# Two layers of graph aggregation on one core: the idle products of the opening changed in form and number, one product by W.T and one addition of the last stage moved

## The chip, the cores and the metric

The kernel runs on one core of a Trainium2 chip. The metric is the device time of one execution in microseconds (us), as the median of three runs; lower is better. The engines are named as the profile names them: PE is the matrix engine (PEld is its weight load), DVE the vector engine, ACT the scalar engine, POOL the third elementwise engine, SP the engine that only issues transfers here. L373 is line 373 of the kernel.

## The reference

`x` is 4096 x 512, `adj` 4096 x 4096 (sparse, diagonal set, never negative), `W` 512 x 512, all float32. Cut to what is computed:

```python
# layer 0
head = (adj > 0); head = head / max(sqrt(row_sum(head * head)), 1e-12)
inc  = adj + head
x    = layernorm(x + (inc @ x) / row_sum(inc))
# layer 1
A2     = adj + I
dscale = diag(A2) ** -0.5
temp   = A2 @ x @ W.T
A_norm = dscale[:, None] * A2 * dscale[None, :]
x      = layernorm(x + relu(A_norm @ temp))
```

The heavy work is three products of a 4096 x 4096 matrix with a 4096 x 512 one: `inc @ x`, `A2 @ x` and `A_norm @ temp`.

## The kernel before, in words

**Tiling and stages.** Blocks are 128 wide, and everything stays in float32. Each heavy product is done by seven half-size products in place of eight (the sums of operands that this needs are made by DVE). Layer 0 takes one such level, layer 1 two. There are 16 pairs of row blocks in layer 0. The first pair is different: the operand sums of `x` are not there yet, so `multiply_plain` (L542) does its products one by one while the inputs are still landing; the pairs after it go through `multiply1` (L529). Layer 1 is a list of 224 steps, of eight steps for each of seven outer products, two column strips and two multiplications (`steps`); each step issues the seven inner products of `multiply2` (L298), and the last step of eight hands the sums to `inner` and `outer`. The order of the work is written out by hand: the program is emitted in the order in which it is to run (`manual_schedule`), and each engine runs its instructions in that order.

**The opening.** SP issues four half loads of the transposed adjacency block `adj_q` (L615), one for each of the chunks c = 0 to 3. For each chunk `count_half` has ACT take the signs (L353; in the last chunk DVE does half, L367), and PE sums them over the partitions by eight products with a matrix of ones, `ones_b` (L373, 128 columns of bf16 each, all accumulated in PSUM bank 7). ACT then takes the root of the count (L357), DVE finishes the scale (L388, L389) and builds the entries of `inc` from it (`to_inc`, L502 and L504), and only then can the first product of `multiply_plain` run. Between the chunks, `idle_products` has PE do products whose result nobody reads: it takes PSUM bank 2 as a new tile for each one, `bank(2)`, so that each such product gets the bank when the product before it has given it back. The number after each chunk is a list by hand, `(0, 3, 0, 5)`. Their moving operand is a piece of the tile of the features that POOL has filled with ones (L621). The loads of `x` (`load_x`, L336 and L337) stand behind one small POOL copy that reads the signs of chunk 0 (L627), and SP issues them one after the other. The signs go to tiles with two buffers (`sr`), so the signs of chunk c + 2 wait for the counts of chunk c.

**The product by W.T.** Once an eighth of a column block of `A2 @ x` is complete, `project` multiplies it by W.T, also by seven small products of 256 columns. It is a generator: it yields a dictionary from place to action, and `multiply2` runs the action of place m just ahead of its inner product m. One project is spread over three steps. The small product (`product`, two matmuls of K = 128, each of which PE runs as two records, L832) takes the one spare PSUM bank, 7, and ACT copies it out (L834); the next small product needs that bank back. The sums `s1` to `s4` of the operands are made by POOL (L839 to L842). Of every two projects that run together, the second (`first` is false) does its products at other places than the first. In the step whose number is 5, `leave_operands` of the project before runs at the places 2 and 4: ACT scales the rows (L881) and issues their stores (L885, L891).

**The last stage.** `finish` does the last four steps of the seventh outer product with its epilogue woven in. `multiply` runs one inner product over the four steps (L996), `quarter` transposes four blocks of a sum by PE (L1000), has DVE add and clip them (`take`, L1008) and measures them (L1011). `deviation` (L1025 on DVE, L1027 on ACT), `invert` (L1030, L1031 on DVE) and `leave` (L1038 on ACT or L1040 on DVE, and a store by SP, L1042) normalise the rows and store them. `add(c21[:, 3, :], acc[q7])` and `add(c21[:, 2, :], acc[q7])` are two DVE additions (L761) of the inner product q7 into two blocks of the last sum; `quarter(1, 1, 1)` transposes the first of them, and `end_rows` (L1085) reads the second. `begin_rows` (L1082) are the products of the last inner product that come between.

## Time and profile before

| | us |
|---|---|
| median of three runs | 2268.39 (2268.12 to 2269.62) |
| the profiled execution, its own time | 2268.52 |
| its span, first to last instruction | 2266.7 |
| PE busy in the span | 2251.2 (99%) |
| DVE busy | 1846.9 (81%) |
| ACT busy | 538.9 (24%) |
| POOL busy | 298.2 (13%) |
| first idle product starts | 8.22 |
| first product of `multiply_plain` starts | 14.58 |

The profile is one execution. A timeline row gives the start, the time from the first start to the last end of the merged group, engine, line, operation, output<-inputs, shape and count; the bracket at the end is the idle time of the engine ahead of it and what ended it. A float32 product of PE shows as two records. The start of one record to the start of the next is what PE is held; the end of a record holds a pipeline's length more, so the durations of neighbours overlap. "PE q L832 <- ACT p L834" in the table of waits means that PE, at line 832, waited for ACT's instruction that writes p at line 834.

### The profile page before, as it was taken

The page shows a single profiled execution, that of the slowest core. Times are in us where ns is not written, and L with a number is a line of the kernel's source. Part 1 is how long each engine was busy: PE and PEld are TensorE (multiplying, and loading weights), DVE is VectorE, ACT ScalarE, POOL GpSimd, SP SyncE. Part 2 cuts the span into 40 slices and gives each one's busy share as a digit, 9 for nine tenths or more (in the row PEclk, how much of TensorE's full clock was granted, in tenths as well). Part 3 has the DMA queues.
Part 4 walks back from the last instruction along what each step waited for, and adds up shares of the span by engine and source line. Part 5 has one row for each costly group of instructions (what it writes and reads, how often), then busy time and mean ns, then how long its engine had stood idle before and what let it go on. Part 6 is the DMA issues. An engine that isn't in the chain of part 4 may idle for free.

```text
span 2266.7 us, 22289 instructions
## 1 busy us (share of the span) xinstructions
PE 2251.2 (99%) x7409; PEld 1387.3 (61%) x7410; DVE 1846.9 (81%) x2629; ACT 538.9 (24%) x1343; POOL 298.2 (13%) x408
## 2 busy tenths in 40 slices
PE   8999999999999999999999999999999999999998
PEld 7888888888888844444555544555544444444444
DVE  6989999989989886888877888887666789767678
ACT  4346546545553000000111100111110011200013
POOL 0111122221112110001112200111310010100001
PEclk9999999999999999999999999999999999999999
DMA  9778888888886575575677767577775677765674
GB/s 309 262 268 288 264 272 276 287 280 285 266 251 224 184 278 220 205 308 192 239 272 232 231 236 274 177 286 276 217 245 218 235 287 282 254 243 211 234 287 172
DMA packets 177044, 568.29 MB, mean 251 GB/s; under 512 B 18064, under 2 KB 54944, under 8 KB 138528
## 3 DMA queue, kind: packets, MB, share of 16 engines
q1 hardware_dynamic: 128832, 459.32, 57.1%
q0 software_dynamic: 32480, 92.85, 13.1%
q10 hardware_dynamic: 15616, 14.69, 2.0%
q8 instruction: 59, 0.97, 0.2%
q14 instruction: 57, 0.47, 0.1%
HBM read 443.04 MB, written 123.74 MB: 250 GB/s over the span
## 4 chain that ended last, share of the span: by engine, by line
PE 91%; DVE 5%; DMA 3%; issue 1%; ACT 0%; SPq 0%; ACTq 0%; POOL 0%; DVEq 0%
PE q L298 54%; PE q L529 32%; PE q L832 4%; DVE s L170 1%; DMA a<-adj_q 1%; DVE r L255 1%; PE q L996 1%; DMA nat<-adj 1%; DMA a<-adj_r 1%; DMA b<-x 1%; PE q L906 1%; DVE s L172 1%; ACT nat L353 0%; DVE ts L273 0%; DVE c L790 0%
## 5 line engine op out<-in xcount | busy, mean ns | idle before, releaser
L298 PE MATMUL q<-s,ts 128*128 128x512 f32 x1320 | 609.6, 592 | 0.2 <-DVE u L752 0.2
L529 PE MATMUL q<-b,s 128*128 128x256 f32 (+1 forms) x1920 | 453.6, 379 | 0.2 <-DVE s L172 0.2
L298 PEld LDWEIGHTS q<-s,ts 128*128 128x128 f32 x1320 | 250.8, 190 | 294.0 <-issue 268.0
L170 DVE TENSOR_TENSOR s<-a 128x1024 f32<-128x1024 f32 x234 | 288.0, 1231 | 164.8 <-PE q L298 138.8
L529 PEld LDWEIGHTS q<-b,s 128*128 128x128 f32 x1920 | 363.2, 189 | 52.0 <-DVE s L172 0.6
L529 PE MATMUL q<-b,a 128*128 128x256 f32 (+1 forms) x1440 | 350.6, 379 | 0.0
L298 PE MATMUL q<-a,tr 128*128 128x512 f32 x688 | 326.7, 593 | 0.0
L529 PEld LDWEIGHTS q<-b,a 128*128 128x128 f32 x1440 | 273.1, 190 | 37.9
L298 PE MATMUL q<-s,tr 128*128 128x512 f32 x440 | 224.8, 592 | 0.0
L298 PEld LDWEIGHTS q<-a,tr 128*128 128x128 f32 x688 | 129.0, 190 | 144.0 <-issue 137.6
L353 ACT ACTIVATE nat<-nat,tiny 128x512 f32<-128x512 f32 x240 | 172.9, 721 | 29.4 <-DMA nat<-adj 23.1
L298 PE MATMUL q<-a,ts 128*128 128x512 f32 x344 | 176.0, 593 | 0.0
L172 DVE TENSOR_TENSOR s<-a,s 128x512 f32<-128x512 f32 x234 | 165.1, 706 | 8.0
L173 DVE TENSOR_TENSOR s<-a,s 128x512 f32<-128x512 f32 x234 | 164.7, 704 | 8.0
L750 ACT COPY p<-q 128x512 f32<-128x512 f32 x27 | 15.7, 583 | 649.3 <-PE q L298 649.3
L504 DVE TENSOR_TENSOR a<-a,mask 128x1024 f32<-128x1024 f32 (+1 forms) x127 | 154.5, 1217 | 6.4
L502 DVE SCALAR_TENSOR_TENSOR mask<-a,sc 128x1024 f32<-128x1024 f32 (+2 forms) x129 | 154.2, 1196 | 2.2
L298 PEld LDWEIGHTS q<-s,tr 128*128 128x128 f32 x440 | 83.7, 190 | 94.8 <-issue 85.0
L414 ACT ACTIVATE nat<-nat 128x512 f32<-128x512 f32 x192 | 118.4, 617 | 13.1 <-DMA nat<-adj 13.1
L298 PEld LDWEIGHTS q<-a,ts 128*128 128x128 f32 x344 | 65.3, 190 | 80.7 <-issue 75.7
L839 POOL TENSOR_TENSOR y<-c,c 128x256 f32<-128x256 f32 x16 | 21.3, 1334 | 641.3 <-DVE c L765 391.5
L170 DVE TENSOR_TENSOR s<-r 128x1024 f32<-128x1024 f32 x48 | 59.8, 1245 | 40.2 <-PE q L298 32.5
(221 smaller groups left out, 2124.1 us busy)
## 6 DMA issues: line engine op xcount, KB each, us to landing
a<-adj_r SPq DMA_DIRECT2D x112, 1024.0 KB, 7.0
a<-oa SPq DMA_DIRECT2D x80, 1024.0 KB, 5.4
nat<-adj SPq DMA_DIRECT2D x240, 256.0 KB, 6.0
a<-adj_q SPq DMA_DIRECT2D x60, 1024.0 KB, 6.3
tr<-ob SPq DMA_DIRECT2D x112, 512.0 KB, 4.0
oa<-r SPq DMA_DIRECT2D x32, 1024.0 KB, 10.1
oa<-sr POOLq DMA_DIRECT2D x60, 512.0 KB, 7.0
y<-x POOLq DMA_DIRECT2D x64, 256.0 KB, 4.9
```

The costliest lines, as they stand in the source:

```text
L170: nc.vector.tensor_add(s[:, S3:S1 + 1, :], a[:, A11:A22 + 1, :], a[:, A21, :].unsqueeze(1).to_broadcast([P, 2, w]))
L172: nc.vector.tensor_add(s[:, S2, :], a[:, A11, :], s[:, S1, :])
L173: nc.vector.tensor_add(s[:, S4, :], a[:, A12, :], s[:, S2, :])
L255: raises.append(lambda: nc.vector.tensor_add(r, r, a))
L298: nc.tensor.matmul(acc[m], left, right, start=(kk == 0), stop=(kk == last))
L353: nc.scalar.activation(y, a, AF.Sign, bias=tiny, scale=2.0 ** 64, accum_out=accum)
L414: nc.scalar.activation(nat, nat, AF.Copy, accum_out=totals[j][:, h, t:t + 1])
L502: nc.vector.scalar_tensor_tensor(m, v, 0.0, s.unsqueeze(1).to_broadcast(list(v.shape)), op0=ALU.is_gt, op1=ALU.mult)
L504: nc.vector.tensor_add(z, z, y)
L529: nc.tensor.matmul(acc[m][:, 0:w], left, b[:, right, 0:w], start=(kk == 0), stop=(kk == NP - 1))
L832: nc.tensor.matmul(ps, left[:, e, :], wt[:, right, e, :], start=(e == 0), stop=(e == 1))
L906: nc.tensor.transpose(ps[:, at + i * P:at + (i + 1) * P], C_of[3][h][d // 2][:, 2 * r + d % 2, cols], ident)
```

## The change

The idle products are done on `ones_b` for both operands, with 128 columns in place of 512, into the first 128 columns of the bank. There are 30 of them ahead of the first chunk, and after the four chunks 2, 10, 0 and 24 in place of 0, 3, 0 and 5. `ones_b` is now filled by DVE and not by POOL, and POOL's fill of the piece of the features is gone. In the second project of a pair, the product of `s2` with T2 moves from place 5 to place 6. In the last stage, the addition into block 3 moves ahead of `invert` and the four stores of `leave`.

```diff
-    nc.gpsimd.memset(ones_b, 1.0)
+    nc.vector.memset(ones_b, 1.0)
...
     def idle_products(times):
         for _ in range(times):
-            nc.tensor.matmul(bank(2), ones_b, idle, start=True, stop=True)
+            nc.tensor.matmul(bank(2)[:, 0:P], ones_b, ones_b, start=True, stop=True)
...
     ps = spare()
-    nc.gpsimd.memset(feats[-1][:, 1, T2, 0:H], 1.0)
-    idle = feats[-1][:, 1, T2, 0:H].bitcast(BF16)
+    idle_products(30)
     for c in range(NC):
         m = count_half(0, c, ps)
...
-        idle_products((0, 3, 0, 5)[c])
+        idle_products((2, 10, 0, 24)[c])
...
-            yield {1: product(a12, B21), 3: product(a22, T4), 5: product(s2, T2)}
+            yield {1: product(a12, B21), 3: product(a22, T4), 6: product(s2, T2)}
...
         deviation(0, 0, 4)
+        add(c21[:, 3, :], acc[q7])
         invert(0, 0, 4)
         for n in range(4):
             leave(0, n, True)
-        add(c21[:, 3, :], acc[q7])
         add(c21[:, 2, :], acc[q7])
```

## The prediction, made before the changed kernel was run

> **What bounds the kernel now.** I read the engines' busy times first, then the busy time by stretch, then PE's waits.

> ```profile
> PE 2251.2 (99%) x7409; PEld 1387.3 (61%) x7410; DVE 1846.9 (81%) x2629; ACT 538.9 (24%) x1343; POOL 298.2 (13%) x408
> ```
> ```profile
> 0.00:14.58 14.58, 7.24 (x40) 4.28 (x41) 2.62 (x7) 6.02 (x7) 2.92 (x31) 1.00 0.86 271
> 14.58:73.70 59.12, 58.89 (x270) 50.27 (x271) 46.80 (x54) 22.18 (x55) 2.00 (x3) 1.00 0.95 326
> 73.70:1000.00 926.30, 926.30 (x3828) 725.39 (x3829) 810.27 (x1138) 350.23 (x943) 147.52 (x214) 1.00 0.77 259
> ```

> The columns are the length of the stretch, then PE, PEld, DVE, ACT and POOL. From 14.58 us, where the first product of layer 0 starts, PE is never idle for more than parts of a us. The table of PE's waits after 14.6 us agrees: 0.5 us for ACT at L832 in two waits, three of 0.2 us, and the 0.6 us ahead of that first product. The chain of waits names loads for most of the time up to 73.7 us, but there PE waits 0.2 us for them, so PE and the loads are equally late and PE has no slack to give away. The end is therefore the moment at which PE starts L542, plus its stream, plus the last stage. What the idle products do to that moment decides.

> ```profile
> 8.22 1.92 PE L379 MATMUL q<-b,ones_b 128*128 128x512 bf16 x3
> 9.93 1.91 PE L373 MATMUL q<-sr,ones_b 128*128 128x128 bf16 x16
> 11.64 2.34 PE L379 MATMUL q<-b,ones_b 128*128 128x512 bf16 x5
> 11.88 0.37 ACT L357 ACTIVATE sc<-q,half_m 128x128 f32<-128x128 f32 x1 [1.49 <-PE q L373]
> ```
> ```profile
> 8.91 0.58 PE L379 MATMUL q<-b,ones_b 128*128 128x512 bf16 x1
> 9.55 0.58 PE L379 MATMUL q<-b,ones_b 128*128 128x512 bf16 x1
> 12.31 0.38 PE L379 MATMUL q<-b,ones_b 128*128 128x512 bf16 x1
> 12.74 0.38 PE L379 MATMUL q<-b,ones_b 128*128 128x512 bf16 x1
> 34.78 1.03 PE L373 MATMUL q<-sr,ones_b 128*128 128x512 bf16 x4
> ```

> Two things are to be seen. **The clock:** 16 counts of 128 columns at 9.93 us are (1.91 - 0.31)/15 = 0.107 us apart (0.31 is one such record), 1.2 columns per ns; four counts of 512 at 34.78 us are (1.03 - 0.38)/3 = 0.217 us apart, 2.4 columns per ns. The trace's record of the granted clock begins at 12.10 us: until then PE ran at half speed, although it had been working since 6.24 us. **The waits:** idle products of 512 columns are 9.55 - 8.91 = 0.64 us apart at the slow clock, where their columns take 4 x 0.107 = 0.43, and 12.74 - 12.31 = 0.43 us apart at the fast one, where the columns take 0.217. Each spends 0.21 us beyond its columns at either clock. The counts, which add into one tile, do not; the idle products, of which each takes bank 2 anew, start only when the one before has ended.

> **The idle products.** The new ones keep `bank(2)` for each product, so I keep the 0.213 us: one costs 0.107 + 0.213 = 0.32 us at the slow clock and 0.054 + 0.216 = 0.27 us at the fast one. Bounds: 0.107, if nothing waited, and 0.64, the old product. Cross-check: a record of 128 columns by itself takes 0.26 us (the first count, at 6.24) and the next idle product starts 0.06 us after the end of the last (9.49 to 9.55).

> The start: DVE has nothing to do before 9.70 us, and ACT and SP issue their first work at 0.72. DVE's fill has no row; I take 0.2 us from POOL's 0.23 for the same tile (between 0.1 and 0.3), 0.05 from its end to the weight load and 0.03 to the matmul, as at 2.52 and 14.55: first product at 1.0.

> Slow clock throughout, starts in us: 30 products from 1.0, the last at 1.0 + 29 x 0.32 = 10.28; the eight counts of chunk 0 from 10.39 (before: 6.24); two products at 11.24 and 11.56; counts of chunk 1 from 11.67; ten products from 12.52 to 15.40; 16 counts from 15.51 to 17.11 (before, the last at 11.53: 5.58 later); 24 products from 17.22 to 24.58; L542 at 24.69. Meanwhile ACT and DVE need 14.58 - 11.53 = 3.05 us from the last count to the data of L542, so 20.16: PE is late, not they. **L542 starts 24.69 - 14.58 = 10.1 us later.**

> Queued behind the waits: the signs of chunk 2 need the buffer of chunk 0, so ACT waits to 11.3 and DVE and ACT for chunk 3 to 12.6; with 1.15 and 0.72 us of signs all are done by 13.4, before PE asks at 15.51. SP's loads of `x` hang on the signs of chunk 0 alone and stay where they are. POOL's two dropped fills (0.23 and 0.34 us) lay in 3.4 us of idle time ahead of L627: nothing gained.

> Then the clock. An idle product streams 0.107 of 0.32 us, a third. The trace shows the clock lifted after 5.86 us (6.24 to 12.10) in which columns streamed for about 5.1, and no stretch at a third. I take it that a third does not lift it, and that L542 starts slow. Its stream runs at half speed until the lift: at most 5.86 us, a loss of 2.9; at least 0, if it was lifted before. I take 2.0. [...]

> What comes back: with everything else early, small stalls of PE vanish that hung on loads, ACT and DVE up to 73.7 us. From one record's start to the next they are 0.08 and 0.11 longer than usual at 16.2 to 16.5 us (DVE at L504), 0.21 at 32.2 (ACT's signs), 0.33 and 0.10 at 73.2 to 73.7 (L172): 0.8 us together. DVE starts 5.6 us late against PE's 10.1 and is busy 46.8 of 59.1 us there: it stays ahead.

> **The product by W.T.**

> ```profile
> 1082.53 0.59 PE L298 MATMUL q<-s,ts 128*128 128x512 f32 x1
> 1082.87 0.37 ACT L834 COPY p<-q 128x256 f32<-128x256 f32 x1 [1.13 <-issue]
> 1083.39 1.10 PE L832 MATMUL q<-wt,y 128*128 128x256 f32 x4 [0.26 <-ACT p L834]
> ```

> The product at place 5 finds bank 7 still unread: ACT has two scalings and three store issues ahead of the copy. From 1082.53 to 1083.39 is 0.86 us where a record holds PE 0.43; with 0.07 on the next record, 0.50. The same at 1468.67: 0.47. One place later is two records, 0.86 us: PE would ask at 1083.82, after the copy's end at 1083.24. Both stalls go: **-1.0 us**. Next late is ACT's copy of the moved product, two inner matmuls (1.72 us) ahead of the next small product, the distance that pairs there already have without a stall. The other six such projects stand without a wait now and pay nothing.

> **The last stage.**

> ```profile
> 2253.29 0.61 DVE L1025 BATCH_NORM_AGGREGATE mv<-st 128x2 f32<-128x24 f32 x4
> 2254.45 0.18 DVE L1030 RECIPROCAL sd<-sd 128x4 f32<-128x4 f32 x1 [0.55 <-ACT sd L1027]
> 2254.74 1.28 DVE L761 TENSOR_TENSOR c<-c,q 128x512 f32<-128x512 f32 x2
> 2255.48 0.66 PE L1000 MATMUL q<-ident,c 128*128 128x128 f32 x4 [0.21 <-DVE c L761]
> 2256.17 0.76 DVE L1008 SCALAR_TENSOR_TENSOR o<-q,y 128x256 f32<-128x256 f32 x2 [0.15 <-PE q L1000]
> ```

> The moved addition falls into DVE's 0.55 us of waiting, but q7's last matmul ends only at about 2254.38. So it runs 2254.4 to 2255.0; the reciprocal and L1031 follow to 2255.4, the second addition to 2256.03. PE's L1000 comes at 2255.1, and L1008 starts at 2256.03 in place of 2256.17: **-0.14 us**, between -0.4 and 0. ACT's four scalings (2.93 us) start 0.55 later and end at 2258.4, before ACT's next work at 2258.8; SP's four stores move with them, well ahead of its last ones.

> **The sum.** 10.1 + 2.0 - 0.8 - 1.0 - 0.1 = +10.2 us on the profiled execution's 2268.5, which stands 0.1 above the median of the runs: **2278.6 us** for the median. With the loss at the clock from 1.0 to 2.9 and the small terms off by half: 2277 to 2280.

> **The rivals.**
> A, the forecast: the clock stays low through the idle products. 0.60.
> B, the products wait for each other, but they lift the clock, after 5.86 us as the counts did, at 6.9 us: then 18 at 0.32 and 12 at 0.27, counts from 9.8, two products, counts to 11.0, ten to 13.5, 16 counts to 14.4, and 24 x 0.27 to 20.7: L542 6.1 us later, not slow itself. 6.1 - 0.8 - 1.1 = +4.2: 2272.6 (2272 to 2273.5). For it: by the records' durations PE looks 0.26/0.32 = 81% busy. Against it: 6.24 to 8.7 us streamed 87% and did not suffice. 0.27.
> C, the other side, faster: the products do not wait for each other. The point is the spacing: 30 products fit into 6.24 - 1.0 = 5.24 us at up to 0.17 us each, and 24 into the 2.74 us from the last count to L542 at up to 0.114. At 0.107 both fit and delay nothing; if they also lift the clock, the last counts run in half the time and L542 starts up to 0.9 us earlier. With -1.1 from the two moves: 2266.4 to 2267.3. Against it: the 0.21 us at both clocks above. 0.10.
> Slower still, by something that I do not see: 0.03.

> **How the numbers follow.** The range takes in A and B, which hold 0.87: 2271.0 to 2281.0. What a measurement of this kernel can tell from no change is about 0.2%, 4.5 us: A is above that bound (2272.9), B on it, split 0.12 above and 0.15 within; C is 0.09 within and 0.01 beyond. Faster 0.01, same 0.24, slower 0.75.

> **What would show it.** In the changed kernel's trace: L379 records of 128 columns 0.32 us apart (C: 0.107; B: 0.27 from about 7 us on); the first count at about 10.4 us in place of 6.24; the last idle product at about 24.6 and L542 just behind it, its first records 0.43 us apart in place of 0.217; no wait at L832 near 1083 and 1468 us; L761 ahead of L1030 in the last stage. PE idle for long between 24.7 and 73.7 us would show that the start was not what counts, and the prediction wrong.

## The result, and the profile after

The changed kernel takes 2280.28 us (median of five runs, 2279.25 to 2280.53); the kernel before, five runs beside it, 2268.59. The ratio is 1.005, with a 95% interval of 1.0039 to 1.0062: slower, by 11.7 us. The profiled execution took 2279.3 us, its span 2277.5.

First the page's line of busy times and the busy time by stretch (length, then PE, PEld, DVE, ACT, POOL), the stretches cut where L542 and L529 start.

```profile
PE 2265.3 (99%) x7468; PEld 1393.0 (61%) x7468; DVE 1847.4 (81%) x2630; ACT 538.8 (24%) x1343; POOL 297.8 (13%) x406
```
```profile
0.00:24.86 24.86, 20.29 (x99) 10.34 (x99) 7.37 (x13) 6.02 (x7) 2.53 (x29) 1.00 0.95 306
24.86:84.53 59.67, 59.67 (x268) 51.12 (x268) 47.16 (x54) 21.39 (x51) 2.91 (x4) 1.00 0.78 268
84.53:1010.80 926.27, 926.27 (x3831) 724.64 (x3830) 804.91 (x1132) 350.77 (x946) 146.59 (x213) 1.00 0.76 259
```

The reader is to see that PE is "busy" for 14 us more than before, of which nearly all is in the first stretch, and that from 24.86 to 1010 us it does not stop at all. Busy is not yet useful: the opening, by PE's timeline:

```profile
1.04 9.57 PE L379 MATMUL q<-ones_b 128*128 128x128 bf16 x30 [1.04 <-DVE ones_b L318]
10.41 1.06 PE L373 MATMUL q<-sr,ones_b 128*128 128x128 bf16 x8
11.26 0.63 PE L379 MATMUL q<-ones_b 128*128 128x128 bf16 x2
11.69 1.06 PE L373 MATMUL q<-sr,ones_b 128*128 128x128 bf16 x8
12.54 3.19 PE L379 MATMUL q<-ones_b 128*128 128x128 bf16 x10
15.53 1.91 PE L373 MATMUL q<-sr,ones_b 128*128 128x128 bf16 x16
17.23 7.67 PE L379 MATMUL q<-ones_b 128*128 128x128 bf16 x24
24.86 15.40 PE L542 MATMUL q<-b,a 128*128 128x258 f32 x61
```

Thirty idle products take 9.57 us, (9.57 - 0.26)/29 = 0.32 apart, while eight counts of the same shape take 1.06. The counts of chunk 0, which came at 6.24, come at 10.41, and L542 comes at 24.86 in place of 14.58.

Where the 10.8 us between the two profiled spans lie, by the starts of the first records of each line and, for the last stage, of the second group of transposes at L1000 (L999 after the change):

| stretch | before | after | difference | forecast |
|---|---|---|---|---|
| to L542 | 14.58 | 24.86 | +10.28 | +10.1 |
| L542 to L529 | 57.92 | 59.67 | +1.75 | +2.0 - 0.4 |
| L529 to L298 | 727.02 | 726.58 | -0.44 | -0.4 |
| L298 to the transposes | 1451.66 | 1450.82 | -0.84 | -1.0 |
| transposes to the end | 15.57 | 15.60 | +0.03 | -0.1 |
| sum | 2266.74 | 2277.53 | +10.8 | +10.2 |

### The profile page after: what moved, and what is told of

Read it like the earlier page. It is cut to its first block, busy times and chain, and to the rows that moved or that the text cites. A ratio compares the mean times of both kernels' runs of the same rounds, so it can differ in the third digit from the quotient of the medians.

```text
span 2277.5 us, 22400 instructions
## 1 busy us (share of the span) xinstructions
PE 2265.3 (99%) x7468; PEld 1393.0 (61%) x7468; DVE 1847.4 (81%) x2630; ACT 538.8 (24%) x1343; POOL 297.8 (13%) x406
## 4 chain that ended last, share of the span: by engine, by line
PE 99%; DVE 1%; issue 0%; ACT 0%; ACTq 0%; DVEq 0%
PE q L298 57%; PE q L529 32%; PE q L831 4%; PE q L542 3%; PE q L995 1%; PE q L379 1%; PE q L905 1%; PE q L373 0%; DVE s L170 0%; DVE c L760 0%; DVE st L1010 0%; DVE st L938 0%; DVE s L172 0%; DVE o L760 0%; PE q L451 0%
## 5 line engine op out<-in xcount | busy, mean ns | idle before, releaser
L298 PE MATMUL q<-s,ts 128*128 128x512 f32 x1320 | 609.5, 592 | 0.2 <-DVE u L751 0.2
L529 PE MATMUL q<-b,s 128*128 128x256 f32 (+1 forms) x1920 | 453.4, 378 | 0.0
L298 PEld LDWEIGHTS q<-s,ts 128*128 128x128 f32 x1320 | 250.4, 190 | 294.4 <-issue 269.8
L529 PEld LDWEIGHTS q<-b,s 128*128 128x128 f32 x1920 | 362.7, 189 | 52.0
L529 PE MATMUL q<-b,a 128*128 128x256 f32 (+1 forms) x1440 | 350.5, 379 | 0.0
L298 PE MATMUL q<-a,tr 128*128 128x512 f32 x688 | 326.7, 592 | 0.0
L529 PEld LDWEIGHTS q<-b,a 128*128 128x128 f32 x1440 | 272.7, 189 | 38.3
L298 PE MATMUL q<-s,tr 128*128 128x512 f32 x440 | 224.7, 592 | 0.0
L298 PEld LDWEIGHTS q<-a,tr 128*128 128x128 f32 x688 | 128.8, 190 | 144.2 <-issue 138.0
L298 PE MATMUL q<-a,ts 128*128 128x512 f32 x344 | 175.9, 593 | 0.0
L172 DVE TENSOR_TENSOR s<-a,s 128x512 f32<-128x512 f32 x234 | 165.1, 706 | 8.0
L504 DVE TENSOR_TENSOR a<-a,mask 128x1024 f32<-128x1024 f32 (+1 forms) x127 | 154.5, 1217 | 6.4
L298 PEld LDWEIGHTS q<-s,tr 128*128 128x128 f32 x440 | 83.6, 190 | 98.4 <-issue 88.7
L298 PEld LDWEIGHTS q<-a,ts 128*128 128x128 f32 x344 | 65.2, 190 | 78.7 <-issue 73.4
L298 PE MATMUL q<-r,tr 128*128 128x512 f32 x192 | 92.2, 592 | 0.0
## 6 DMA issues: line engine op xcount, KB each, us to landing
oa<-r SPq DMA_DIRECT2D x32, 1024.0 KB, 10.3
```

The costliest lines, as they stand in the source:

```text
L172: nc.vector.tensor_add(s[:, S2, :], a[:, A11, :], s[:, S1, :])
L298: nc.tensor.matmul(acc[m], left, right, start=(kk == 0), stop=(kk == last))
L504: nc.vector.tensor_add(z, z, y)
L529: nc.tensor.matmul(acc[m][:, 0:w], left, b[:, right, 0:w], start=(kk == 0), stop=(kk == NP - 1))
```

## The experiments

Each starts from the changed kernel or from the kernel before, as its edit shows. None leaves out work whose result is used.

### One tile for all idle products

```diff
-            nc.tensor.matmul(bank(2)[:, 0:P], ones_b, ones_b, start=True, stop=True)
+            nc.tensor.matmul(idle_bank[:, 0:P], ones_b, ones_b, start=True, stop=True)
...
+    idle_bank = bank(2)
     idle_products(30)
```

> All idle products of the changed kernel write one tile of bank 2, taken once. If it is the wait of each product for the bank that costs (my theory), they run 0.107 us apart, the 30 end at about 4.3 us, the first count is back at about 6.2 us and the first L542 at 13.7 to 14.6 us; the time is 2266.3 to 2267.6 us, a little below the kernel before. If it is the number of products, or the switch of a product's start and stop, that sets the spacing (rival), they stay 0.32 us apart and the time stays at 2279 to 2281 us.

Measured: 2266.97 us (2266.52 to 2269.69), the kernel before beside it 2267.52; ratio 0.9998 (0.9989 to 1.0007). Some rows of PE's timeline of the opening:

```profile
1.04 3.38 PE L379 MATMUL q<-ones_b 128*128 128x128 bf16 x30 [1.04 <-DVE ones_b L318]
6.34 1.01 PE L373 MATMUL q<-sr,ones_b 128*128 128x128 bf16 x8 [1.92 <-ACT sr L353]
10.85 1.50 PE L379 MATMUL q<-ones_b 128*128 128x128 bf16 x24
13.76 12.56 PE L542 MATMUL q<-b,a 128*128 128x258 f32 x56 [1.40 <-issue]
```

The same thirty products take 3.38 us, (3.38 - 0.31)/29 = 0.106 apart. Number, shape and place are those of the changed kernel; only the taking of the bank differs. So the wait of each product for the one before it is the whole of the loss, as far as the measurement can tell. The rival C of the prediction (no wait, 2266.4 to 2267.3 us) fails on that wait alone: this run is what C would have been.

### The thirty alone, and eight in place of 24

```diff
-        idle_products((2, 10, 0, 24)[c])
+        idle_products((0, 0, 0, 0)[c])
```

> The changed kernel with the 30 products ahead of the first chunk alone, none between and after the chunks. My theory: the 30 run 0.32 us apart to 10.4 us, counts of chunks 0 and 1 follow to 12.1; the signs of chunks 2 and 3 wait for the two buffers that these counts free, so the last count starts at about 14.3 us and the first L542 at about 17.3 us, 2.7 later than before, with up to 2 us lost at the slow clock: 2269.5 to 2272.0 us. If the whole delay came from the 30: L542 at 24 us and 2279 us or more. If it came from the 24 at the end alone: no change from before.

Measured: 2271.51 us (2270.95 to 2272.84), ratio to the kernel before 1.0019 (1.0009 to 1.0029). PE's rows behind the thirty:

```profile
10.41 1.91 PE L373 MATMUL q<-sr,ones_b 128*128 128x128 bf16 x16
12.75 1.72 PE L373 MATMUL q<-sr,ones_b 128*128 128x128 bf16 x16 [0.43 <-ACT sr L353]
17.21 9.08 PE L542 MATMUL q<-b,a 128*128 128x258 f32 x33 [2.74 <-issue]
```

The 0.43 us of waiting for ACT ahead of chunk 2's counts is the queue named in the prediction: the signs of chunk 2 wait for the buffer that the late counts of chunk 0 free. With the thirty alone L542 is 2.6 us late.

```diff
-        idle_products((2, 10, 0, 24)[c])
+        idle_products((2, 10, 0, 8)[c])
```

> The changed kernel with 8 products after the last chunk in place of 24. My theory: they end at 19.8 us, and ACT's and DVE's 3.05 us from the last count to the data, to 20.2 us, become what the first L542 waits for: L542 at 20.2 us, 4.7 earlier than in the changed kernel, low clock at its start as there: 2274.5 to 2277 us. If the 24 cost nothing since the data came as late (rival): 24.9 us and 2279 to 2280.5 us. If their whole length counted, with no data path behind it: 24 - 8 = 16 products, 5.1 us, L542 at 19.7 us.

Measured: 2276.05 us (2275.64 to 2276.31), ratio 1.0037 (1.0022 to 1.0051). PE's last two rows of the opening:

```profile
17.23 2.55 PE L379 MATMUL q<-ones_b 128*128 128x128 bf16 x8
20.18 6.12 PE L542 MATMUL q<-b,a 128*128 128x258 f32 x15 [0.39 <-DVE a L504]
```

Now L542 waits 0.39 us for DVE, at 20.18: the path through ACT and DVE from the last count. Sixteen products fewer (5.1 us) bring L542 4.7 us forward, not 5.1. So of the 10.3 us, 5.6 are the late counts and 4.7 the 24 products beyond the data.

### What lifts the clock

The prediction took it that products streaming a third of the time do not lift the clock. To test how much streaming does, the products got 512 columns and kept their wait:

```diff
+    ones_w = w1_pool.tile([P, D], BF16, name="ones_w", bufs=1)
+    nc.vector.memset(ones_w, 1.0)
-            nc.tensor.matmul(bank(2)[:, 0:P], ones_b, ones_b, start=True, stop=True)
+            nc.tensor.matmul(bank(2), ones_b, ones_w, start=True, stop=True)
-    idle_products(30)
+    idle_products(15)
-        idle_products((2, 10, 0, 24)[c])
+        idle_products((1, 5, 0, 12)[c])
```

> The changed kernel with idle products of 512 columns that wait for the bank, 0.64 us apart, streaming 67% of the time, and so many that they last as long: 15, then 1, 5, 0 and 12. If the share that streams lifts the clock (under 0.69 not, over 0.78 so): low clock through the 15, lift at the end of the first window that takes in the counts of chunks 0 and 1, between 12 and 16 us, then 0.43 us apart, first L542 at 20 to 23 us, not slow itself; 2272 to 2276 us. If waiting products never lift it: low until after 25 us, 2279 to 2281 us. If the time in which a record is open lifts it (0.91 here, 0.82 with 128 columns): lift by 4 to 7.5 us, first L542 at about 18 to 19 us, 2270 to 2273 us.

Measured: 2272.5 us (one run); the clock was lifted at 11.75 us, L542 started at 20.24. The time alone would fit the first and the third account; the lift and the start of L542 fit the first alone, with the lift a little early: the 3.41 us ahead of it, 8.34 to 11.75 us, held a part of the fifteen and the counts of chunk 0 (eight in 1.01 us, from 10.93), not yet those of chunk 1 (eight in 0.61 us, from 11.98).

In the traces, the record of the granted clock begins at the first lift, and the edges that follow stand multiples of 3.41 us apart: 3.41 and 3.41 us with the thirty alone (14.18, 17.59, 21.00), 3.41 and 6.82 with one tile and no moves (4.76, 8.17, 14.99); from the lift to the fall at the end it is 2252.80 us in the kernel before and 2245.97 in the changed kernel, twice 3.41 less. How much of the 3.41 us ahead of a lift PE streamed can be estimated from the records, each counted as the time of its columns at the granted rate (0.107 us for 128 columns at the slow clock, not the 0.26 us for which the record is open): about 0.75 in the run above (8.34 to 11.75 us), 0.81 with the thirty alone (10.77 to 14.18), 0.86 in the kernel before (8.68 to 12.10) and 0.99 in the changed kernel (25.37 to 28.79). In the changed kernel 3.41 us with 0.69 (15.13 to 18.55) brought no lift. These estimates are good to some 0.02. From which share on the clock is lifted, and over what time the share counts, the runs do not show. The share of time in which a record was open does not sort these cases: it was 0.92 in the stretch of the changed kernel that brought no lift (PE busy 3.13 of 3.41 us), and 0.87 with the thirty alone, where the lift came. That speaks against rival B, which counted open records as busy. The fall back shows in two runs. The thirty alone, in three stretches from edge to edge (length, PE's busy time with its records, granted clock, share of the DMA engines, GB/s):

```profile
14.18:17.59 3.41, 0.67 (x7) 1.00 1.09 367
17.60:21.00 3.40, 3.40 (x10) 0.50 1.09 352
21.01:24.42 3.41, 3.41 (x18) 1.00 1.10 363
```

The clock is lifted at 14.18 us, while the counts run. In the 3.41 us after that PE is busy for 0.67 us, and idle for 2.74 us ahead of L542; the next 3.40 us are granted half speed, and ten records run in them where the following stretch runs 18 (a row also counts the records that only begin or end in the stretch: at half speed 3.41/0.43 = 8, at full speed 3.41/0.217 = 16). A reader should note that the clock column shows 1.00 also before the first lift, where the trace has no record: there the clock is read from the spacing alone (16 counts of 128 columns are 0.107 us apart in the kernel before, ahead of the lift).

### More products in one tile

```diff
-    idle_products(30)
+    idle_bank = bank(2)
+    idle_products(46)
-        idle_products((2, 10, 0, 24)[c])
+        idle_products((3, 14, 0, 24)[c])
```
(with `idle_bank` for `bank(2)` as in the first experiment)

> The idle products write one tile of bank 2, 46 ahead of the first chunk and 3, 14, 0 and 24 after the chunks; both moves stay. If a share of streaming of 0.78 or more in one 3.41 us window lifts the clock, 46 products 0.107 us apart (4.9 us) hold such a window in nearly every phase: clock lifted by 7.5 us, first L542 at 13.3 to 13.8 us in every execution, 2266.3 to 2267.3 us and a narrower spread than the kernel before. If the early lift is worth nothing (rival, since the signs of chunk 3 come at 10.4 us in any case): as the version with 30, 2266.5 to 2267.5, with the same spread of over 3 us.

Measured: 2267.03 us (2266.36 to 2271.37), the kernel before beside it 2267.67; ratio 1.0 (0.9991 to 1.0009). The clock is lifted at 6.38 us (eight counts take 0.64 us from 6.28, where slow ones take 1.01) and L542 starts at 13.71, as expected, but the runs spread over 5 us: half of the expectation failed. What spreads the runs of this kernel is shown only in part: where L542 starts early, PE can wait for a load of `x` behind it, 0.17 us in this run's profile and 0.94 in that of the two moves alone (L542 at 13.87). Whether that makes the slowest runs was not tried; what else it is stays open. Neither version with one tile is faster than the kernel before by more than the measurement can tell.

### The two moves alone, and the kernels once more

The kernel before with the two moves and nothing else:

> The kernel before with the two moves alone (product of s2 at place 6, addition ahead of the reciprocal). My theory: the two stalls of PE at L832 near 1083 and 1468 us, 0.5 us each, are gone and nothing takes their place: PE reaches the last stage 1.0 us earlier, and the last stage gives 0.0 to 0.3 us more; 2267.3 to 2267.7 us. Rival: the stalls come back at the next copy or at the next step's sums, or the last stores eat the gain: 2268.4 to 2268.8 us.

Measured: 2267.50 us (2266.64 to 2268.34) against 2267.52 beside it; ratio 0.9999 (0.9990 to 1.0008). The number expected was met, but the kernel before read 1.1 us lower beside it than in its first five runs, so the difference is the rival's: none that can be told.

The changed kernel with the moves undone (`5: product(s2, T2)`, the addition behind `leave`):

> The changed kernel with the two moves undone, the idle products kept. If the parts add up: 1.0 to 1.3 us above the changed kernel, 2280.3 to 2281.8 us, with the first L542 at 24.9 us as there. If the moves did nothing in the changed kernel, because its late start had removed those stalls already: 2279.2 to 2280.5 us, and no wait at L832.

Measured: 2279.54 us (2279.36 to 2281.18), ratio to the kernel before 1.0053 (1.0037 to 1.0068): not to be told from the changed kernel by its time. Its profile has one stall at L831 behind ACT's copy (0.3 us, near 1095) and one of 1.4 us behind DVE at L789, of which more below.

The kernel before once more, unchanged:

> The kernel before, once more with a profile. From PE's first L298 record to the transposes of the first block of the last stage (the second group at L1000) it took 1451.66 us, the kernels with the moves and no stall of DVE near 1060 us took 1450.55 to 1450.93. My theory: the stalls at L832 (0.4 to 0.5 us each) are there again, one or two of them, and the stretch takes 1451.0 us or more. Rival: they were chance of one execution, and the stretch takes 1450.6 us. From those transposes to DVE's last instruction 11.24 us, and to the end of the span 15.57 if the end of the first profile was the rule, 15.88 if it was an exception.

Measured: 2266.81 us (one run). PE's waits in the whole span:

```profile
PE q L373 <- ACT sr L353: 6.3, 2, 6.1
PE q L542 <- DVE a L504: 0.8, 1, 0.8
PE q L1000 <- DVE c L761: 0.2, 1, 0.2
PE q L298 <- DVE u L752: 0.2, 1, 0.2
```

No wait at L832 at all, and 1450.55 us from L298 to the transposes: the rival was right, the two stalls came and went with the execution. The wait for DVE c L761 in the last stage is there again, and so are 11.24 us from the transposes to DVE's last instruction and 15.57 to the end.

The version with one tile and 30 products, without the moves:

> The version with one bank tile and 30 products, without the two moves. Theory: one or two stalls of 0.4 to 0.5 us at L832 are back, near 1082 or 1467 us, the stretch from the first L298 to the second group of transposes takes 1451.0 us or more in place of 1450.68, and from there to DVE's last instruction 11.24 us in place of 10.96. Rival: 1450.7 and 10.96, the moves change nothing.

Measured: 2268.64 us (one run), one stall at L832:

```profile
1467.18 1.02 PE L298 MATMUL q<-s,ts 128*128 128x512 f32 x2
1468.44 0.89 PE L832 MATMUL q<-wt,y 128*128 128x256 f32 x3 [0.24 <-ACT p L834]
```

1451.30 us to the transposes and 11.24 from there to DVE's last instruction, as the theory had it. Its opening, in four stretches with the same columns as above, shows the clock lost and lifted again:

```profile
4.77:8.17 3.40, 1.52 (x25) 1.00 0.96 335
8.18:11.58 3.40, 2.63 (x27) 0.50 0.95 300
11.60:14.99 3.39, 3.21 (x24) 0.50 1.04 355
15.00:18.41 3.41, 3.41 (x17) 1.00 1.08 361
```

It was first lifted at 4.76 us, in the time of the thirty products and the pause behind them (they end at 4.42). In the next 3.40 us PE was busy for 1.52, and two stretches at half speed followed.

The changed kernel once more:

> The changed kernel once more, with a profile and on the same chip as the others of this call. If the phase of the 3.41 us window is the only chance in its start: L379 and the first L542 at the same times to 0.05 us (24.86), the clock lifted 2.3 to 5.5 us after that, and the time within 2278.5 to 2281.0 us. If the start itself varies, L542 is elsewhere.

Measured: 2280.01 us (2278.51 to 2280.36), ratio to the kernel before 1.0054 (1.0037 to 1.0071). L542 starts at 24.86 as before; the clock is lifted 5.75 us later, at 30.61, a quarter of a us beyond what was expected; in the first profile it was 3.93 us later, at 28.79. By the two pairs of profiles the change costs 2277.53 - 2266.74 = 10.8 and 2278.15 - 2265.03 = 13.1 us.

## Why the prediction was right, point by point

**The wait for the bank** was right, and it carried the result: 0.32 us apart, as worked out from the old products' 0.64. The start at 1.0 was 1.04 (DVE's fill took 0.17 us, not 0.2). L542 was forecast at 24.69 and came at 24.86.

**PE has no slack**: shown by the table of stretches. After L542 no stretch gave back more than 0.84 us.

**The clock** was right in kind: it stayed low through 24 us of waiting products, and from the second to the ninth the records of L542 are 0.43 us apart (the first gap is 0.56). The size differed between executions: 1.9 us lost in the first profile of the changed kernel (lifted at 28.79), 2.9 in the second (30.61), and 1.4 in the kernel with the moves undone, whose opening is the same (lifted at 27.60), against the 2.0 that was the author's choice between the bounds 0 and 2.9. That 2.0 met the first profile so closely is luck.

**The stalls up to 73.7 us** were booked at 0.8 and gave 0.63 (0.19 in L542's stretch, 0.44 behind it). One of them was misread: the 0.21 us at 32.2 us was no stall. That row has three products at L373 where the program issues four, and the trace of before has 39 matmuls at L373 beside 40 weight loads: a record is missing, and the gap is its time.

```profile
L373 PEld LDWEIGHTS <-ones_b x40: 94/147/152, 2.5 to 35.2; 128*128 128x128 bf16 x40
L373 PE MATMUL q<-sr,ones_b x39: 264/312/379, 6.2 to 35.4; 128*128 128x128 bf16 x32, 128*128 128x512 bf16 x7
```

The stall behind L542's stretch was right in kind, and its size differs between executions. From L529 to L298 all six profiles in which L542 starts at 17.2 us or later take 726.58 us; the six in which it starts at 14.6 or earlier take 726.64 to 727.38, and the second profile of the kernel before is the one with 726.64.

**The product by W.T** is the term that was mis-sized. "Both stalls go: -1.0 us" was right for the one profile and not for the kernel. Four profiles without the move have two, none, one and one such stalls; eight with the move have none. By these profiles the move is worth 0 to 1.0 us and about 0.5 on average, which no comparison of times here can tell. That it works as described is seen in the changed kernel: the copy ends at 1094.76, and PE asks at 1095.34.

```profile
1094.39 0.37 ACT L833 COPY p<-q 128x256 f32<-128x256 f32 x1 [1.14 <-issue]
1094.48 1.02 PE L298 MATMUL q<-s,tr 128*128 128x512 f32 x2
1095.34 0.38 PE L831 MATMUL q<-wt,y 128*128 128x256 f32 x1
```

**The last stage** was forecast at -0.14 us. Some rows of DVE's timeline of the changed kernel:

```profile
2265.16 0.69 DVE L760 TENSOR_TENSOR c<-c,q 128x512 f32<-128x512 f32 x1 [0.52 <-PE q L995]
2265.77 0.17 DVE L1029 RECIPROCAL sd<-sd 128x4 f32<-128x4 f32 x1
2266.05 0.68 DVE L760 TENSOR_TENSOR c<-c,q 128x512 f32<-128x512 f32 x1
2266.65 0.75 DVE L1007 SCALAR_TENSOR_TENSOR o<-q,y 128x256 f32<-128x256 f32 x2
```

The order is as described. From the transposes to DVE's last instruction all eight moved kernels take 10.96 us and all four unmoved ones 11.24: -0.28. At the end of the span it is gone against the kernel before (15.60 against 15.57 twice), and there against the two other unmoved ones (15.88). From DVE's last instruction to the end of the span it is 0.3 us less in the program of before than in every other one (4.33 us against 4.64 in the changed kernel); why was not tried and stays open.

**The sum** of +10.2 us met 10.8 in the first pair of profiles, 11.7 between the medians and 13.1 in the second pair. So the median of 2280.28 us lies inside the range of 2271 to 2281 and 0.3 us above the narrower 2277 to 2280. In the first pair every term is within 0.2 us of its forecast. In the second pair the 2.9 us that are lacking are 1.05 between L542 and L529 (the later lift), 0.98 at the product by W.T, 0.40 in the opening (the kernel before reached L542 at 14.36), 0.34 from L529 to L298 and 0.14 at the end: the prediction paid the change for stalls that the kernel before has in some executions only, and the later lift of the clock added most of the rest.

## What to carry to other kernels

An idle product cost its spacing here, not its columns: with the buffer taken anew for each, each waited for the one before (0.32 us apart, against 0.106 in one tile), and with 66 of them the first product of the work itself came 10.3 us later. Keep them in one tile, count them by the gap that they fill, and look which engine is late when they end. A stall that one profile shows is a gain only if a second profile of the same kernel shows it too, and a gap between records is first checked against the number of records that the program issues.

## What the runs showed of the hardware that was not expected

Near 1060 us DVE comes late to L789 in two of the twelve profiles: PE waited 1.4 us for it in the changed kernel without the moves and 0.9 in the one with eight last products, and not at all in either profile of the changed kernel. What decides this was not followed.
